# Side work placed anew in a two-layer attention kernel: table portions, block ends, norm steps and an iteration's scaling

## The chip, the core and the metric

The kernel runs on one core of a Trainium2 chip. The metric is device microseconds of one execution. The core has engines that each work through their own list of instructions in order: TensorE (PE in the profile, with PEld for its weight loads), VectorE (DVE), ScalarE (ACT), GpSimd (POOL), and SyncE (SP), which here only issues DMAs. An instruction whose operands are not ready holds up everything behind it on its engine. So the place of an instruction in its engine's list matters as much as its length.

## What is computed

Two layers over x of shape (2, 512, 64, 32), that is 2 batches of 2048 tokens with 512 channels, 8 heads of 64, all in float32:

```python
# layer 0: full attention, q and k with 64 more channels of frequency and time embeddings
q, k = [x, emb] @ Wq, [x, emb] @ Wk;  v = x @ Wv
o = softmax(q k^T / 8) v
x1 = x + o @ Wout + bout
# layer 1: normalization, Nystrom attention (256 landmarks), quantized feed-forward
n = layernorm(x1);  q, k, v = n @ Wqkv
qL, kL = means of 8 tokens each
A = softmax(qL kL^T);  z = 6 steps of an iterative pseudo-inverse of A
o = softmax(q kL^T) (z (softmax(qL k^T) v)) + conv(v)
x2 = x1 + o @ Wout1 + bout1
out = x2 + layernorm(x2) @ (dequantized table @ W)
```

The feed-forward weight is a 512 x 512 array of 4-bit indices into a table of 16 levels, with a scale for 64 elements each. One step of the pseudo-inverse is z <- z (13 - xz (15 - xz (7 - xz))) / 4.

## The kernel before

The tokens of a batch are cut into four blocks of 512, the channels into four chunks of 128 partitions, and the heads are worked in pairs (two heads of 64 fill 128 partitions). There are 8 pairs: two batches of four. The order of the work is written by hand: Python generators yield after each unit of work, and loops advance them at set places. TensorE's list is therefore what the source says, step by step, and so are those of VectorE, ScalarE and GpSimd. The order of SyncE's DMAs is set by a planner.

**First layer.** `attention0` walks the 64 steps of a pair (four blocks of queries times 16 chunks of keys) in groups of two. A group does the scores (L1258), their exponentials on ScalarE (L1266), VectorE's additions for the row sums (L1276), and the values matmuls (L1288) of the group before. Every eight groups a block ends: an addition into q_f (L1295), the row sums on TensorE (L788), a reciprocal (L1303), a DMA that spreads it, and GpSimd's multiplication (L1306).

The next pair's work stands between these groups. At the groups named in `BURSTS[n]` a filler is advanced up to its next REST: projections of q and k (with their combined weights, L989 to L992, and evictions L1018 and L1023), value projections (L1126), and at the end two reductions of |q| and |k| with a bound (L1114, L1116). In any other group one entry of the list `soon` is run (a token sum L900, a finish step), or else one portion of `feed_forward_map`, which makes the feed-forward weight from the table: for each of four chunks a conversion of the indices (L1342 to L1347), 14 levels (a comparison L1352 and an addition L1353), a scaling (L1357); at the end the products mp (L1364) and the store of the result. One portion stood in each such group whose number is not a multiple of 8, and one beside each value projection but those of pair 0.

For n = 4, the first pair of batch 1, the finish of batch 0's first layer is the filler too: out units (matmuls yp_f, eviction into xr_f L1148) and the norm's steps. Those are: sums L1159/L1160, mean L1163, subtraction L1164, squares L1167/L1170 on ScalarE, additions L1175/L1176, variance L1179, square root L1181, reciprocal L1198, and two multiplications, GpSimd's L1201 and VectorE's L1202.

**Between the layers** the string `ORDER` sets the turns: m is one product of the second layer's projections (L2072, eviction L2082), n a norm step, o an out unit.

**Second layer.** The loop `for n, pair in enumerate(todo)` (L2402) runs the pseudo-inverse of one pair. `iteration_start` scales A into M (L1766 to L1774). Each step of `pinv` (L1800) squares M, then R: a flip by TensorE (L1796) that ScalarE copies back (L1797), the products (L1806), and subtractions by VectorE (L1819). Between the steps `chunk(c)` places the next pair's scores and values (attn3, L1635) and the previous pair's last attention (attn1: scores L1863, exponentials L1868, sums L1872, values L1879, row sums L788, reciprocal L1892, L1899, L1900). Between the three last products (wp L1781, tp L1790) `last(i)` places more. In both, `advance(finish)` places single steps of batch 0's or 1's finish: out units yp_g, norm steps as above (reciprocal L1928), and units of the feed-forward fp_g (L1962, with L1951 and L1952). A last string (L2546) sets the turns of the end.

TensorE's results lie in PSUM banks: four in turn for most work (`bank`) and two for the products of the iteration (`product_bank`).

Of the kernel before, what the change touches and what calls it, by code (L numbers as in the profile page):

```python
# [13 lines left out]
ALU = mybir.AluOpType  # L14
# [23 lines left out]
def general_path(  # L38
# [618 lines left out]

BAND = P + 2 * HALO

ORDER = "1mononmmnomomnnm2mnoonmnmnmoonmn3mmnoonmnmmnoommnnmnmmnmmnmmnmmmmnmmmmmn"  # L660

GAP = object()
REST = object()

FEW = (2, 1), (1, 2), (1, 1), (2, 2)
BURSTS = (
    *[(1, 6, 14, 23)] * 3, (4, 10, 17, 25), (1, 3, 6, 10, 12, 15, 18, 20, 23, 26, 28, 31),
    (4, 12, 21), (4, 12, 21), (12, 22),
)

# [2 lines left out]
def fast_path(  # L673
# [241 lines left out]
    class Heads0:  # L915
# [139 lines left out]
        def units(self, xbs, parts, after=None, ready=None):  # L1055

            self.xbs = xbs
            self.begin()
            values = self.values()
            if self.b == 0:  # L1060
                for kind in "q" if self.plain else "qk":
                    self.few(kind)
                self.embed(4)
                yield
                yield REST
            if self.plain:
                for i, (kind, t) in enumerate(self.uses):
                    if i == 2 and self.b == 0:
                        self.few("k")
                        self.embed(2)  # L1070
                    if kind == "q" and self.b:
                        if t == 0:
                            yield from values
                            while not ready():
                                yield GAP
                    if kind == "q" and t == 0:
                        self.queries()
                    self.project(kind, t)
                    yield
                if after:  # L1080
                    after.begin()
            else:
                self.queries()
                if self.b and self.hp == 0:
                    for m in range(2):
                        next(values)
                        yield
                    parts[0].begin()
                    yield REST
                if not self.ws:  # L1090
                    self.combine_w()
                    for _ in range(2):
                        next(values)
                        yield
                while ready and not ready():
                    yield GAP
                for tp in range(2):
                    yield from self.products(tp, parts[tp], parts[1] if tp == 0 else after)
            if self.next:
                self.next.load()  # L1100
                if self.next.b:
                    self.next.embed(4)
            for _ in values:
                if self.hp or self.b:
                    advance(ffn_map)
                yield
                if self.next and not self.next.plain and not self.next.ws:
                    self.next.combine_w()
            if self.next:
                self.next.load("v")  # L1110

            big = small.tile([P, 2], F32, tag="big0", name=f"big_{self.name}")
            for i, m in enumerate((self.q, self.k)):
                nc.vector.tensor_reduce(big[:, i : i + 1], m, AX.X, ALU.max, apply_absolute_value=True)  # L1114
            i = self.b * NPAIR + self.hp
            nc.vector.scalar_tensor_tensor(  # L1116
                bound[:, i : i + 1], big[:, :1], D**-0.5, big[:, 1:], ALU.mult, ALU.mult
            )
            yield

    def values_of_tokens(v, t, xb, w_of, name):

# [123 lines left out]
    def attention0(hd, filler, needed, bursts, beside=None):  # L1246
# [62 lines left out]
        for i in range(0, len(steps) + 1, GROUP):  # L1309
            group = [(step, scores(*step)) for step in steps[i : i + GROUP]]  # L1310
            for step, p in group:
                add(step, p)
            for step, p, its_acc in pending:
                values(step, p, its_acc)
            pending = [(step, p, acc) for step, p in group]
            burst = i // GROUP in bursts
            if burst:
                advance(filler, len(steps), True)
            if not group:
                while needed in filler:  # L1320
                    advance(filler)
            if late:
                sums(*late)
                late = None
            if soon and not burst:
                soon.pop(0)()
            elif beside and not burst and i // GROUP % 8:
                advance(beside)

    def feed_forward_map():  # L1330
# [8 lines left out]
        for k in range(KC):  # L1339
            nc.sync.dma_start(qi, qidx[k * P : (k + 1) * P, :])  # L1340
            yield
            nc.vector.tensor_copy(qf, qi)  # L1342

            nc.vector.tensor_scalar(hits[:, 0, :], qf, 0.0, float(len(NF4)), ALU.is_lt, ALU.mult)
            nc.vector.tensor_tensor(qf, qf, hits[:, 0, :], ALU.add)
            nc.vector.tensor_scalar(qf, qf, 0.0, float(len(NF4) - 1), ALU.max, ALU.min)
            nc.vector.tensor_scalar(wl[:, k, :], qf, 0.0, NF4[0], ALU.is_equal, ALU.mult)  # L1347
            yield
            for i, level in enumerate(NF4):
                if i and level:  # L1350
                    hit = hits[:, i % 4, :]
                    nc.vector.tensor_scalar(hit, qf, float(i), level, ALU.is_equal, ALU.mult)  # L1352
                    nc.vector.tensor_tensor(wl[:, k, :], wl[:, k, :], hit, ALU.add)  # L1353
                yield
            for j in range(C // 64):
                blk = wl[:, k, j * 64 : (j + 1) * 64]
                nc.vector.tensor_scalar(blk, blk, sc_sb[:, k, j : j + 1], None, ALU.mult)  # L1357
        wff_sb = block_of(lpool, "wo", "wff_f")
        nc.sync.dma_start(wff_sb, chunked(wffT))
        yield  # L1360
        for m in range(KC):
            mp = bank(f"mp1_{m}")
            for k in range(KC):
                nc.tensor.matmul(  # L1364
                    mp, lhsT=wl[:, k, m * P : (m + 1) * P], rhs=wff_sb[:, k, :], start=k == 0, stop=k == KC - 1
                )
            nc.scalar.copy(tmp[:, m, :], mp)
            yield
        nc.sync.dma_start(mT_d, tmp)
        yield  # L1370

    def load_wo(w, name):
# [599 lines left out]
    def finish1_units(b, os, early):  # L1972
        for t in range(NTB):
            if t == NTB - 1 and early:
                f = early.pop()
                yield from f.out_units()
                yield from f.norm_units()
                yield from f.map_units(lambda m, name: bank(name))
                return
# [22 lines left out]
        after = parts_for(others[0])[0] if others and not (n and plain(n)) else None  # L2002
        return heads[n].units(xbs, None if plain(n) else parts_for(n), after, ready)

    ffn_map = [feed_forward_map()]
    cur = heads[0]
    cur.w = w0_first
    drain(units_of(0))
# [1 line left out]
    for n, (b, hp) in enumerate(todo[:-1]):  # L2010
# [12 lines left out]
        if n == 3:  # L2023
            while ffn_map:
                advance(ffn_map)
            wo_sb = load_wo(wo0, "wo_f0")
            write_bands()
        if hp == NPAIR - 1:
            last_oTs, oTs = oTs, []
# [368 lines left out]

    finish, early = [], []
    for n, pair in enumerate(todo):  # L2402
        before = todo[n - 1] if n else None
        after = todo[n + 1] if n + 1 < len(todo) else None
# [4 lines left out]
        if n == NPAIR + 3:  # L2409

            xb = as_block(kvpool.tile([P, NST, P], F32, tag="v", name="xb_g_early"))
            xn = lambda: block_of(lpool, "xn", "xn_g_early")
            early.append(Finish1(1, NTB - 1, [p.o for p in todo[:NPAIR]], xb, xn, True))
            before.load_o(late_buffer(f"o2_{n - 1}"))
        pair.iteration_start()
        while vals:
            advance(vals)
        if after:
# [4 lines left out]
        if n:  # L2423
            q = late_buffer if n > NPAIR + 1 else lambda name: kvpool.tile([P, S], F32, tag="k", name=name)
            pair.prefetch1(q(f"q2_{pair.name}"))

        def chunk(c):
            nonlocal landmarks
            if before and 0 < c <= n_ones:
                before.attn1_end(c - 1)  # L2430
            if n == NPAIR and c == 1:

                finish.append(finish1_units(1, [p.o for p in todo[:NPAIR]], early))
            advance(finish)
            if c == NTB:
                if after:
                    landmarks = after.landmarks_values()
                    next(landmarks)
                    drain(convolution(n + 1))
                else:  # L2440
                    advance(finish, 2)
                return
            ones_before = before if c < n_ones else None
            if ones_before:
# [2 lines left out]
                    before.attn1_scores(c, 1)  # L2447
                before.attn1_add(c)
            if after:
                for s, bank_of in ((2 * c, product_bank), (2 * c + 1, bank)):  # L2450
                    after.attn3_scores(s, bank_of)
                    after.attn3_add(s)
            else:
                advance(finish)
            if ones_before:
                before.attn1_values(c)
            if after:
                after.attn3_values(2 * c)
            else:
                advance(finish)  # L2460
            if after:
                after.attn3_values(2 * c + 1)
            if ones_before:
                before.attn1_sums(c)
                before.attn1_inverse(c)
            if n == NPAIR + 2 and c % 2:
                advance(finish)

        def last(i):
            nonlocal start  # L2470
# [24 lines left out]
            if i == 5:  # L2495
                pair.attn1_scores(0, 0)
                pair.attn1_scores(0, 1)
            advance(finish)

        landmarks = start = None  # L2500
        n_ones = NTB if n + 2 < len(todo) else NTB - 1
# [41 lines left out]


    ones_last = last_attn1()
    for c in "1f1ffnf11f1ff1afafff1f1f1f1faas11bs1bs1bbt":  # L2546
        if c == "f":
            advance(finish)
        elif c == "n":
# [111 lines left out]
```

## Time and profile before

| | us |
|---|---|
| median of 3 runs | 2706.99 |
| lowest, highest run | 2700.99, 2707.6 |
| the profiled execution's own time | 2700.81 |
| its span in the profile | 2699.0 |

The mean granted TensorE clock of the profiled execution is 0.997. The stages, with busy times in us (times from the span's start):

| stage | start to end | PE | DVE | ACT | POOL |
|---|---|---|---|---|---|
| first projections | 0 to 56 | 52.2 | 17.4 | 5.6 | 0.2 |
| attention of pair 0 | 56 to 182 | 123.6 | 106.0 | 50.1 | 15.4 |
| pair 1 | 182 to 341 | 153.6 | 137.0 | 66.8 | 17.2 |
| pair 2 | 341 to 500 | 153.7 | 136.2 | 66.6 | 17.7 |
| pair 3 | 500 to 660 | 159.6 | 132.2 | 69.5 | 7.4 |
| pairs 4 to 7 | 660 to 1390 | 723.6 | 497.1 | 304.5 | 45.8 |
| between the layers | 1390 to 1710 | 309.7 | 224.0 | 86.1 | 20.0 |
| iterations of pairs 0 to 5 | 1710 to 2310 | 595.6 | 297.6 | 177.9 | 28.8 |
| pair 6 | 2310 to 2440 | 125.3 | 78.8 | 35.6 | 7.4 |
| pair 7 | 2440 to 2530 | 85.3 | 47.7 | 19.6 | 6.1 |
| the end | 2530 to 2699 | 158.1 | 100.7 | 25.4 | 6.8 |

The profile's rows name a source line, an engine, an operation, and its output and inputs. Row numbers such as L1806 are lines of the kernel before. A bracket at a row's end gives the idle time of that engine just before it and what ended it. Idle time of an engine that isn't the bottleneck costs nothing by itself.

### The profile page before, as it was taken

Reading aid. Unit: us, or ns where it says so; the run is one execution under the profiler, and the core shown is the slowest. Engines: PE = TensorE matmul, PEld = TensorE weight load, DVE = VectorE, ACT = ScalarE, POOL = GpSimd, SP = SyncE. Lnnn points to the kernel's source line nnn. Section 1 sums busy time; section 2 is a strip of 40 time slices with the busy share of each in tenths; the row PEclk is TensorE's granted clock in tenths of the full one; section 3 lists DMA queues with packets and bytes.
Section 4 is the critical chain, followed back from the end, with each engine's and each line's share of the span. In section 5 each row is a group of like instructions: output and inputs, shape, how many; then the busy total and the mean of one; then the engine's idle time right before and its main releaser. Section 6 shows DMA issues by size and latency. Waiting matters only on the chain.

```text
span 2699.0 us, 41317 instructions
## 1 busy us (share of the span) xinstructions
PE 2640.4 (98%) x16898; PEld 1346.8 (50%) x16898; DVE 1774.5 (66%) x2253; ACT 907.5 (34%) x1356; POOL 172.8 (6%) x127
## 2 busy tenths in 40 slices
PE   9999999999999999999999999999999999999998
PEld 5343433444344434343344455777677666655344
DVE  4898888976557677767668856544644645465565
ACT  1344344443343335345422223223333222231210
POOL 0101010000001100000002000000000000000000
PEclk9999999999999999999999999999999999999999
DMA  4101011201221210020114633213111113021211
GB/s 134 38 13 45 13 36 44 75 21 52 86 79 59 78 52 13 24 85 29 45 61 170 229 109 114 90 33 125 49 37 60 61 42 105 28 79 36 90 39 48
DMA packets 124759, 177.16 MB, mean 66 GB/s; under 512 B 16912, under 2 KB 78096, under 8 KB 122000
## 3 DMA queue, kind: packets, MB, share of 16 engines
q1 hardware_dynamic: 118416, 153.15, 18.0%
q0 software_dynamic: 5440, 20.97, 2.1%
q8 instruction: 134, 2.20, 0.3%
q14 instruction: 65, 0.53, 0.1%
q10 hardware_dynamic: 704, 0.31, 0.0%
HBM read 94.02 MB, written 63.57 MB: 58 GB/s over the span
## 4 chain that ended last, share of the span: by engine, by line
PE 85%; DVE 10%; issue 2%; ACT 1%; DMA 1%; SPq 0%; POOL 0%; DVEq 0%; ACTq 0%; POOLq 0%
PE sc_f L1258 13%; PE av_f L1288 13%; PE pa L1806 5%; PE pb L1806 5%; DVE acc_f L1276 5%; PE vp L1126 4%; PE vp_f L1126 4%; PE fp_g L1962 4%; PE yp_g L1141 4%; PE yp_f L1141 3%; PE pc_f L1003 3%; PE pu L2072 3%; PE sc L1863 2%; PE sc L1635 2%; PE av L1656 2%; PE av L1879 2%
## 5 line engine op out<-in xcount | busy, mean ns | idle before, releaser
L1266 ACT ACTIVATE p_f<-sc_f 128x1024 f32<-128x1024 f32 x512 | 496.5, 1021 | 583.2 <-PE sc_f L1258 581.6
L1276 DVE TENSOR_TENSOR acc_f<-acc_f,p_f 128x1024 f32<-128x1024 f32 x448 | 577.0, 1288 | 133.8 <-ACT p_f L1266 106.4
L1258 PE MATMUL sc_f<-q_f,k_f 64*64 64x512 f32 x4096 | 490.4, 593 | 2.6 <-ACT p_f L1266 2.6
L1288 PE MATMUL av_f<-p_f,v_f 64*64 64x512 f32 x4096 | 485.2, 589 | 0.0
L1288 PEld LDWEIGHTS av_f<-p_f,v_f 64*64 64x64 f32 x4096 | 157.0, 133 | 283.1 <-issue 282.4
L1258 PEld LDWEIGHTS sc_f<-q_f,k_f 64*64 64x64 f32 x4096 | 148.5, 133 | 284.3 <-issue 262.6
L1806 PE MATMUL pa<-M 128*128 128x192 f32 (+1 forms) x640 | 153.4, 385 | 5.6 <-ACT M L1797 5.6
L1806 PE MATMUL pb<-R 128*128 128x192 f32 (+1 forms) x640 | 149.3, 380 | 0.0
L1306 POOL TENSOR_TENSOR q_f<-q_f,rinv_f 128x512 f32<-128x512 f32 x32 | 51.2, 1600 | 1123.2 <-DMA rinv_f<-acc_f 880.1
L1806 PEld LDWEIGHTS pa<-M 128*128 128x128 f32 x640 | 109.3, 195 | 27.2 <-ACT M L1797 8.7
L1126 PEld LDWEIGHTS vp_f<-wv_f,x 128*128 128x128 f32 x1024 | 115.7, 192 | 8.9 <-issue 8.9
L1806 PEld LDWEIGHTS pb<-R 128*128 128x128 f32 x640 | 106.6, 190 | 23.3 <-DVE M L1819 0.3
L1141 PE MATMUL yp_f<-q_f,wo_f 128*128 128x512 f32 x256 | 113.2, 596 | 4.2 <-DVE xr_f L1148 4.2
L1126 PE MATMUL vp_f<-wv_f,x 128*128 128x128 f32 x1024 | 117.3, 276 | 0.0
L1141 PE MATMUL yp_g<-o,wo_f 128*128 128x512 f32 x256 | 114.8, 598 | 0.0
L1126 PE MATMUL vp<-w,xh 128*128 128x128 f32 x896 | 105.9, 277 | 0.0
L1126 PEld LDWEIGHTS vp<-w,xh 128*128 128x128 f32 x896 | 102.1, 192 | 4.9 <-issue 3.0
L1819 DVE SCALAR_TENSOR_TENSOR M<-M,pb 128x320 f32<-128x320 f32 (+1 forms) x160 | 60.1, 417 | 60.7 <-PE pb L1806 60.7
L1962 PE MATMUL fp_g<-xn_g,mT 128*128 128x512 f32 (+1 forms) x232 | 99.8, 580 | 0.0
L1900 POOL TENSOR_TENSOR o<-o,rinv 128x512 f32<-128x512 f32 x32 | 46.0, 1436 | 815.8 <-DVE rinv L1899 673.2
L1868 ACT ACTIVATE p<-sc 128x512 f32<-128x512 f32 x128 | 66.6, 602 | 93.4 <-PE sc L1863 93.2
L1819 DVE SCALAR_TENSOR_TENSOR R<-M,pa 128x320 f32<-128x320 f32 (+1 forms) x160 | 58.5, 407 | 49.5 <-PE pa L1806 49.4
(278 smaller groups left out, 3204.4 us busy)
## 6 DMA issues: line engine op xcount, KB each, us to landing
xh<-xh_fd SPq DMA_DIRECT2D x12, 1024.0 KB, 5.9
rinv_f<-acc_f SPq DMA_DIRECT2D x256, 32.0 KB, 1.9
xr_f<-in_x_dram SPq DMA_DIRECT2D x8, 1024.0 KB, 5.1
x_fd<-xr_f POOLq DMA_DIRECT2D x8, 1024.0 KB, 4.9
xh_fd<-xn_f POOLq DMA_DIRECT2D x8, 1024.0 KB, 4.6
k<-k_fd SPq DMA_DIRECT2D x8, 1024.0 KB, 6.1
rinv<-acc SPq DMA_DIRECT2D x256, 32.0 KB, 1.8
x<-in_x_dram SPq DMA_DIRECT2D x7, 1024.0 KB, 6.0
```

The costliest lines, as they stand in the source:

```text
L1003: nc.tensor.matmul(to, lhsT=w[:, k, :], rhs=x[:, k, :], start=start and k == 0, stop=k == 1, skip_group_check=True,)
L1126: nc.tensor.matmul(vp[:, j * P : (j + 1) * P], lhsT=xb[:, k, j * P : (j + 1) * P], rhs=w_of(k), start=k == 0, stop=k == KC - 1,)
L1141: nc.tensor.matmul(yp, lhsT=wo_sb[:, k, m * P : (m + 1) * P], rhs=oTs[k][:, toks], start=k == 0, stop=k == NPAIR - 1,)
L1258: nc.tensor.matmul(sc[r * D : (r + 1) * D, h, :], lhsT=hd.k[rows, lo : lo + D], rhs=hd.q[rows, t * TB : (t + 1) * TB], start=True, stop=True,)
L1266: nc.scalar.activation(p, sc, AF.Exp, scale=D**-0.5)
L1276: nc.vector.tensor_tensor(acc, first if c == 1 else acc, p, ALU.add)
L1288: nc.tensor.matmul(av[r][half, :], lhsT=hd.v[keys, c, half], rhs=pp[keys, h, :], start=c == 0, stop=c == NST - 1,)
L1806: nc.tensor.matmul(dst, lhsT=lhsT[:, k, t * P : (t + 1) * P], rhs=rhs[:, k, :], start=k == 0, stop=k == 1)
L1819: nc.vector.scalar_tensor_tensor(out, m, scale, pr, ALU.mult, ALU.subtract)
L1868: nc.scalar.activation(p[:, h, :], sc, AF.Exp, scale=D**-0.5)
L1962: nc.tensor.matmul(fp[:, cols], lhsT=mT[:, k, m * P : (m + 1) * P], rhs=self.xn[:, k, cols], start=k == 0, stop=k == KC - 1,)
L2072: nc.tensor.matmul(to, lhsT=w[:, k, :], rhs=x[:, k, :], start=start and k == 0, stop=k == 1, skip_group_check=True)
```

## The change

No instruction of arithmetic is added or taken away; the change moves work on the engines' lists, and one choice of banks.

- **Table portions.** A portion stands in the groups of `TABLE` alone, and `NVS` = 3, 3, 3, 1 portions stand beside a pair's four value projections (and three beside each of pair 4's first two). A conversion is two portions. The load of the out weight `wo_f0` stands right behind the store of the finished map.
- **The bound's reductions.** That of |q| stays; that of |k| and the bound go to `soon`.
- **BURSTS[4].** From the fourth burst on, most are one group earlier, so that an out unit stands right behind a block's row sums (groups 9, 17, 25).
- **ORDER.** The same steps in other turns; the last norm's reciprocal and multiplications ahead of two small sums and a weight's combination.
- **TURNS.** Where pairs 4 to 7 of the second layer had a finish step at fixed places, a table says how many (f), and where the out units of the last block (o) stand. The squares no longer stand ahead of a flip's copy.
- **`iteration_start`** of the next pair at the end of the present one, ahead of that turn's finish step.
- **Banks of attn3's scores.** The plain bank first and the product bank second, where it was the other way, if c is 0 or no pair is before.
- **TAIL.** Two letters of the last string move by a few places.

```diff
-ORDER = "1mononmmnomomnnm2mnoonmnmnmoonmn3mmnoonmnmmnoommnnmnmmnmmnmmnmmmmnmmmmmn"
+ORDER = "1omnonmmnomomnnm2mnoonmnmnmoomnnm3mnoonmnmmnoomnnmnmmmnmnmmmnmmmmnmnmmmm"
+TURNS = (
+    (",,,", "f,,,", "f,,,", "f,,,", "f,", "f,f,f,f,f,"),
+    ("f,,,", "ff,,,", "f,,,", "f,,,", "f,", "f,f,f,f,f,f"),
+    ("fff,,,", "ff,,,", "f,,,", "f,,,", "ff,", ",f,f,f,f,"),
+    ("fffoo,,,", "f,f,f,", "f,f,f,", "ff,,oo,", "f,", ",f,,f,f,ff"),
+)
+TAIL = "11fffnf11f1ff1afafff1f1f1f1faas11bsbs11bbt"
+TABLE = 9, 10, 11, 12, 16, 17, 18, 19, 20, 21, 22, 25, 27
+NVS = 3, 3, 3, 1
...
-    *[(1, 6, 14, 23)] * 3, (4, 10, 17, 25), (1, 3, 6, 10, 12, 15, 18, 20, 23, 26, 28, 31),
+    *[(1, 6, 14, 23)] * 3, (4, 10, 17, 25), (1, 3, 6, 9, 11, 14, 17, 19, 22, 25, 27, 30),
...
                     for m in range(2):
                         next(values)
+                        advance(ffn_map, 3)
                         yield
...
-            for _ in values:
-                if self.hp or self.b:
-                    advance(ffn_map)
+            for i, _ in enumerate(values):
+                advance(ffn_map, NVS[i])
                 yield
...
+            def most(i, m):
                 nc.vector.tensor_reduce(big[:, i : i + 1], m, AX.X, ALU.max, apply_absolute_value=True)
+            def both_of_them():
+                most(1, self.k)
...
+            most(0, self.q)
+            soon.append(both_of_them)
...
-            elif beside and not burst and i // GROUP % 8:
+            elif beside and not burst and i // GROUP in TABLE:
                 advance(beside)
...
             nc.vector.tensor_tensor(qf, qf, hits[:, 0, :], ALU.add)
+            yield
...
         nc.sync.dma_start(mT_d, tmp)
+        loaded.append(load_wo(wo0, "wo_f0"))
...
-        pair.iteration_start()
+        if not n:
+            pair.iteration_start()
...
+        def turn(c, i):
+            for turn in TURNS[n - NPAIR][c].split(",")[i] if n >= NPAIR else "":
+                if turn == "f":
+                    advance(finish)
+                else:
+                    next(outs_early[0])
...
-            advance(finish)
+            turn(c, 0)
...
-                for s, bank_of in ((2 * c, product_bank), (2 * c + 1, bank)):
+                kinds = (product_bank, bank) if c and before else (bank, product_bank)
+                for s, bank_of in zip((2 * c, 2 * c + 1), kinds):
...
                 pair.attn1_scores(0, 1)
-            advance(finish)
+                if after:
+                    after.iteration_start()
+            turn(NTB + 1, i)
...
-    for c in "1f1ffnf11f1ff1afafff1f1f1f1faas11bs1bs1bbt":
+    for c in TAIL:
```

More of the change, by code (lines that the diff above doesn't have):

```diff
@@ L1112, in units @@
             big = small.tile([P, 2], F32, tag="big0", name=f"big_{self.name}")
-            for i, m in enumerate((self.q, self.k)):
+            def most(i, m):
                 nc.vector.tensor_reduce(big[:, i : i + 1], m, AX.X, ALU.max, apply_absolute_value=True)
[L1115 to L1119, printed above, removed]
+            def both_of_them():
+                most(1, self.k)
+                i = self.b * NPAIR + self.hp
+                nc.vector.scalar_tensor_tensor(
+                    bound[:, i : i + 1], big[:, :1], D**-0.5, big[:, 1:], ALU.mult, ALU.mult
+                )
+            most(0, self.q)
+            soon.append(both_of_them)
     def values_of_tokens(v, t, xb, w_of, name):
@@ L1360, in feed_forward_map @@
         yield
+        yield
+        yield
         for m in range(KC):
@@ L1975, in finish1_units @@
                 f = early.pop()
-                yield from f.out_units()
+                yield from outs_early[0]
                 yield from f.norm_units()
@@ L2003, in units_of @@
         return heads[n].units(xbs, None if plain(n) else parts_for(n), after, ready)
-    ffn_map = [feed_forward_map()]
+    loaded, ffn_map = [], [feed_forward_map()]
     cur = heads[0]
@@ L2025, in fast_path @@
                 advance(ffn_map)
-            wo_sb = load_wo(wo0, "wo_f0")
+            wo_sb = loaded.pop()
             write_bands()
@@ L2397, in fast_path @@
     todo[0].prefetch1(kvpool.tile([P, S], F32, tag="k", name="q2_first"))
-    finish, early = [], []
+    finish, early, outs_early = [], [], []
     for n, pair in enumerate(todo):
@@ L2413, in fast_path @@
             early.append(Finish1(1, NTB - 1, [p.o for p in todo[:NPAIR]], xb, xn, True))
+            outs_early.append(early[0].out_units())
             before.load_o(late_buffer(f"o2_{n - 1}"))
-        pair.iteration_start()
+        if not n:
+            pair.iteration_start()
         while vals:
@@ L2439, in chunk @@
                     drain(convolution(n + 1))
-                else:
-                    advance(finish, 2)
+                turn(c, 1)
                 return
@@ L2449, in chunk @@
             if after:
-                for s, bank_of in ((2 * c, product_bank), (2 * c + 1, bank)):
+                kinds = (product_bank, bank) if c and before else (bank, product_bank)
+                for s, bank_of in zip((2 * c, 2 * c + 1), kinds):
                     after.attn3_scores(s, bank_of)
                     after.attn3_add(s)
-            else:
-                advance(finish)
+            turn(c, 1)
             if ones_before:
@@ L2458, in chunk @@
                 after.attn3_values(2 * c)
-            else:
-                advance(finish)
+            turn(c, 2)
             if after:
@@ L2465, in chunk @@
                 before.attn1_inverse(c)
-            if n == NPAIR + 2 and c % 2:
-                advance(finish)
+            turn(c, 3)
         def last(i):
@@ L2497, in last @@
                 pair.attn1_scores(0, 1)
-            advance(finish)
+                if after:
+                    after.iteration_start()
+            turn(NTB + 1, i)
         landmarks = start = None
```

## The prediction

> **What bounds the kernel now.** First the page's busy times, then TensorE's waits by releaser, then the timeline at each wait.
>
> ```profile
> PE 2640.4 (98%) x16898; PEld 1346.8 (50%) x16898; DVE 1774.5 (66%) x2253; ACT 907.5 (34%) x1356; POOL 172.8 (6%) x127
> ```
>
> TensorE (PE) is busy for 2640.4 of 2699.0 us at a mean granted clock of 0.997. The change adds and removes no arithmetic, so it can only win from TensorE's idle time, 50.9 us between matmuls and 7.8 us behind the last, and from matmuls that ran at a low clock. The rest of this text is about whom TensorE waits for (total us, times, longest):
>
> ```profile
> PE pc_f L1003 <- DVE k_f L1018: 9.7, 7, 2.9
> PE pa L1806 <- ACT M L1797: 5.6, 2, 4.2
> PE yp_f L1141 <- DVE xr_f L1148: 4.2, 2, 2.1
> PE rs_f L788 <- DVE acc_f L1276: 3.5, 3, 2.1
> PE wp L1781 <- DVE R L1819: 3.2, 2, 2.1
> ...
> PE sc L1550 <- DVE L L1518: 2.5, 1, 2.5
> PE sc L1635 <- DVE M L1819: 2.2, 10, 0.2
> ```
>
> Nearly all are waits for VectorE (DVE) which has work in front of what TensorE needs, though it is busy for only 66% of the span: an order too late, not an engine too small. Below, "->" is from a wait before to my wait after, in us.
>
> **Table portions, reduces, bursts (first layer).** A steady group of two steps costs TensorE 3.43 us (four batches near 1.7) and VectorE two adds, 2 x 1.29 less overlap = 2.48, so a group has 0.95 free. A level (L1352 + L1353) costs 1.07 from start to start, more than the 0.95: portions in consecutive groups make a backlog, and the next burst of projections waits for its k_f eviction. Value projections (14.6 us of TensorE each head) leave VectorE idle:
>
> ```profile
> 168.37 0.42 DVE L1352 TENSOR_SCALAR hits_f<-tmp_f 128x512 f32<-128x512 f32 x1
> 168.82 0.69 DVE L1353 TENSOR_TENSOR wl_f<-wl_f,hits_f 128x512 f32<-128x512 f32 x1
> ...
> 173.02 2.28 DVE L1114 TENSOR_REDUCE big_f<-q_f 128x1 f32<-128x2048 f32 x1
> ...
> 181.83 1.23 DVE L1276 TENSOR_TENSOR acc_f<-p_f,p_f 128x1024 f32<-128x1024 f32 x1 [4.14 <-ACT p_f L1266]
> ```
>
> The 4.14 at the end is VectorE idle before the first add. The change puts ten portions here: for head 0's end 6 levels (6.42), the weight combination (1.47), a scaling (1.30), a conversion (2.45) and one reduce (2.20) make 13.84, ending at 182.2 against 181.83: 0.4 late. The k reduce with its bound (2.44) follows in the next free group, against four levels fewer later (4.28).
> - Heads 0 to 2, bursts at group 6 in heads 1 and 2: 2.93 and 2.67 -> 0, since no portion is left in groups 1 to 8 (before: one in each free group). Bursts at 14: 1.61, 0.90, 0.22 -> 0: one portion less (1.07) and its free 0.95 make 2.0 us.
> - Head 0, group 6: the k reduce now stands in group 5 behind the token sums: 0.78 -> 3.2. A loss.
> - Row sums at the ends: 1.24 -> 0.5, 2.15 -> 0.15, 0.16 -> 0.
> - Together 12.66 -> 3.85: **8.8 us**. The table's beginning beside head 0's own values costs nothing: VectorE was idle there for 8.73 us before the first add at 56.0.
> - Head 4: the out projections wait (2.13, 2.10) for xr_f evictions behind the reciprocal L1198 (3.33). One group earlier, L1198 falls in the idle time before the row sums, and the out unit has some 1.2 us to spare: -> 0. Of 0.56, 0.11 and 0.62 there remains 0.28. **5.2 us**. SP's wo_f load moves ahead of the loop's end, right behind the table's store; in that queue row-sum spreads stand behind it, but its buffer's last readers (the mp matmuls) are done before the store, so it holds nobody.
>
> **ORDER between the layers.** Moving one pu or eviction ahead empties 1.60 and 0.14; mean and part come 1.1 us sooner for the sc wait (2.53 -> 1.4), and 2.24 -> 1.75. 1.26, 0.86, 0.56 and 0.99 keep their releasers. [...]
>
> ```profile
> 1473.19 3.38 POOL L1201 TENSOR_TENSOR xn_f<-xn_f,rstd_n 128x1024 f32<-128x1024 f32 x1 [12.62 <-DVE rstd_n L1198]
> 1474.28 2.44 DVE L1518 TENSOR_SCALAR L<-L 128x256 f32<-128x256 f32 x1
> ```
>
> L1518 alone takes 0.29 (at 1478.48); beside GpSimd's multiply it ends only when that does. [...] then bringing L1198 and L1202 forward brings the block (2.15) with them, whatever stands behind it pays, and 2.24 stays 2.24 (part: 2.8 us). By the row of a conversion beside GpSimd in head 1 (four instructions 0.7 to 0.85 late each, no full block) half would go, 1.1 (part: 3.9). I take 0.5: **3.3 us**, ends 1 and 5.
>
> **Score banks and scaling.** Ten waits of 0.22 (sc L1635) are for the bank that the last product still holds; the first score then takes a fresh one: **2.2 us**, ends 0 and 2.2. The next iteration's scaling (L1770 to L1774, 1.6 us of VectorE) stands ahead of the finish step L1148, which waited for its projection: 1.20 -> 0, **1.2 us**. Behind it nothing is late: that turn ends with matmuls of 3.7 us.
>
> **Finish steps by table.** The largest single wait:
>
> ```profile
> 2482.74 2.28 DVE L1164 TENSOR_TENSOR xn_g<-xb_g,mean_g 128x2048 f32<-128x2048 f32 x1
> 2485.05 1.06 ACT L1167 ACTIVATE sq_g<-xn_g 128x1024 f32<-128x1024 f32 x1 [5.45 <-DVE xn_g L1164]
> 2486.01 1.13 ACT L1170 ACTIVATE sq_g<-xn_g 128x512 f32<-128x512 f32 x2
> 2487.05 0.24 ACT L1797 COPY M<-p_pa 128x128 f32<-128x128 f32 x1
> 2487.35 1.44 PE L1806 MATMUL pa<-M 128*128 128x320 f32 x2 [4.22 <-ACT M L1797]
> ...
> 2488.79 3.62 PE L1806 MATMUL pa<-M 128*128 128x192 f32 x8
> ```
>
> ScalarE (ACT) serves in order: the squares wait for L1164, and the 0.24 us flip copy that the iteration needs stands behind them. In the changed program squares come one chunk later, behind a flip copy, and two out units of the last block (7.4 us of matmuls) cover L1164: 4.22 -> 0. The matmuls behind took 3.62 where they take 1.89 elsewhere; with the next ones 2.6 us are lost to the clock. The windows show it:
>
> ```profile
> 240.00:246.00 6.00, 4.89 (x12) 2.17 (x13) 3.73 (x6) 0.00 (x0) 3.07 (x3) 1.00 0.14 51
> 2488.00:2493.00 5.00, 5.00 (x16) 3.76 (x15) 1.96 (x6) 0.53 (x2) 0.00 (x0) 0.56 0.00 0
> ```
>
> (start:end, length, busy times, then granted clock, DMA share, GB/s). A wait of 2.93 left the clock at 1.00, 4.22 brought 0.56. [...] But behind the 2.53 wait at 1478.83 the clock was 0.60, and about 1.5 us went. [...]
> - Pair 4 to 5: squares off the flip, 1.43 -> 0.
> - Pair 6: the squares' adds (1.28 + 0.69) leave the place before R, and L1928 (3.35) no longer stands before R's subtraction: 2.06 + 1.19 -> 0, less 0.5 for a chunk in which VectorE has 8.4 us of work against 8.7.
> - Pair 7, gains: 4.22 + 2.6. New waits: its fp units no longer stand between wp and tp, so the two later wp each wait for the add or the subtraction, 0.75 + 0.75. The variance now stands just ahead of the last block's scores: sqrt (0.69) with a table load (1.28) before and after it keeps ScalarE from the exponentials, and the fourth score needs the bank that the first one frees: 1.25. Net 4.05.
> - Together 1.4 + 2.75 + 4.05 = **8.2 us**, ends 3 and 10.
>
> **Tail string.** Two waits, 1.56 (rinv behind L1159/L1160) and 1.51 (var_g), -> one of 1.45: the mean's matmul, now right behind the scores, waits for the last fp unit's two additions and L1159/L1160: **1.6 us**. From 2600 on nothing moves, and the 7.8 us end stays.
>
> **Sum.** 8.8 + 5.2 + 3.3 + 2.2 + 1.2 + 8.2 + 1.6 = 30.5 us. The profiled execution took 2700.81 us (span 2699.0 and 1.8 around it): 2670.3. The runs shown lie at 2700.99, 2706.99 and 2707.6, so the profiled one is like the lowest; I put the forecast 3 us above the sum, half way to the median's 6: **2673 us**, 1.2% less.
>
> **Rivals.**
> - *The cover doesn't hold in the iterations* (pairs 5 to 7): the new waits of pair 7 and pair 6 eat all 8.2, with the scaling's 1.2, and bursts of heads 0 to 2 keep half (4.4): 30.5 - 13.8 = 17 us, 2684 to 2690. For it: in pair 7 three waits are added by hand count. Against: the larger waits go for a reason seen in the trace.
> - *The waits only move*: behind each wait removed the next releaser is as late. Less than 8 us, 2693 to 2707. For it: VectorE is 88 to 98% busy in the second to fourth slices of the page. Against: in the value projections it idles for 4 us.
> - *Slower: a VectorE backlog at the twelve bursts and row sums of heads 0 to 2.* Portions now stand at groups 16 to 22 in a row and at 25 and 27; with the k reduce put into a free group, a backlog of one level and one reduce (1.07 + 2.44 = 3.5) may reach TensorE each time. It decides from about 3.6 us each: 12 x 3.6 = 43 against 12.66 before eats the 21.7 of the other parts and 9 more. Beyond 4.2 each would add 2.6 of clock, 12 x 6.8 = 82: 2748. Against: groups 5 to 8 and 13 to 15 are free to recover 0.95 each.
> - *It does not do what it says*: the instruction order of the two programs excludes this; every move above stands in it.
>
> **Chances.** Forecast 0.66 (2662 to 2682); iteration cover fails 0.18; waits move 0.10; slower 0.05; larger gain than all ends 0.01. A measurement of this kernel tells some 0.3%, 8 us, from no change. Faster 0.85, same 0.10, slower 0.05. The low end is the sum of the upper ends (30.5 + 1.5 + 1.7 + 1.8 + some of the 3.85 left = 38) from the lowest run of 2701, some 2662, and 1 below it; the upper end takes in the first rival: 2692.
>
> **What will show it.** No wait of pc_f for k_f over 1 us after 200 us; pc_f at about 80 us near 3; no pa wait for ACT M; sc L1635 gone from the list; clock 1.00 around 2460; waits of wp for R near 0.75 twice and one of sc for the exponentials near 1.25 in pair 7. A TensorE idle sum over 40 us would make me wrong, or one at the low clock.

## The result

| | before, us | changed, us |
|---|---|---|
| median of 5 runs each (before: the 3 shown ahead and 2 more) | 2704.54 (2700.99 to 2707.6) | 2663.84 (2662.55 to 2665.19) |
| profiled execution, its span | 2700.81, 2699.0 | 2662.55, 2660.7 |
| TensorE idle up to its last matmul, summed over the trace | 50.9 | 20.5 |
| TensorE busy | 2640.4 | 2632.5 |

The ratio is 0.9849 (95% interval 0.9835 to 0.9864). The forecast was 2673 us in a range of 2661 to 2692, so it was right in its sign and its range, and 9 us short. The page's busy times after, and TensorE's waits by releaser (us in total, times, longest):

```profile
PE 2632.5 (99%) x16898; PEld 1345.3 (51%) x16898; DVE 1770.9 (67%) x2253; ACT 907.7 (34%) x1356; POOL 171.7 (6%) x127
```

```profile
PE pc_f L1014 <- DVE k_f L1029: 3.2, 2, 3.0
PE pu L2093 <- DVE s L1499: 2.3, 3, 1.1
...
PE mean_g L1180 <- DVE xn_g_early L1177: 1.5, 1, 1.5
PE sc L1884 <- ACT p L1889: 1.5, 2, 0.8
...
PE wp L1802 <- DVE R L1840: 0.8, 2, 0.4
```

Line numbers of the changed kernel are 11 to 21 higher: pc_f L1014 was L1003. Seven waits of pc_f became two, one of them the 3.0 of head 0, where 3.2 was forecast; the wait of pa for ScalarE's flip copy is gone, and so are yp_f's and the long ones of wp. Of the ten waits of sc L1635 nine are gone; the tenth (now L1656, 0.22 at 2348) stands in a last chunk, where the banks were not swapped. The instructions that count as busy are the same in number on each engine, so the 38.3 us come from two sources: 30.4 of idle time and 7.9 of busy time. The second is where the forecast was short.

To see where the time went, TensorE's two lists were laid side by side, and the clock time of the same count of matmuls was compared. The difference is the second column; the third is from the experiments, each of which takes the part back, compared with the changed kernel in the same way, with the start of the span left out.

| part | forecast | traces, before to after | part taken back |
|---|---|---|---|
| first layer: portions, reduces, bursts | 14.0 | 12.6 | 15.7 |
| ORDER | 3.3 | 5.5 | 7.3 |
| score banks | 2.2 | 6.3 | 6.3 |
| scaling, finish steps, last string | 11.0 | 12.7 | 14.4 |
| start (x arriving) | 0 | 1.1 | |
| sum | 30.5 | 38.2 | |

The start is no doing of the change: the first waits for the time embedding and for x are 0.67 and 1.42 before, 0.36 and 0.35 after, and one and the same program below started once with none and once with 1.44. The third column adds up to more than the second because three of the four kernels met low clocks that the kernel before had not met at those places, some 1.6 us each; the section on the clock shows such falls.

### The profile page after: what moved, and what is told of

It reads as the page before. It is cut to its first block, busy times and chain, and to the rows that moved or that the text cites. A ratio compares the mean times of both kernels' runs of the same rounds, so it can differ in the third digit from the quotient of the medians.

```text
span 2660.7 us, 41330 instructions
## 1 busy us (share of the span) xinstructions
PE 2632.5 (99%) x16898; PEld 1345.3 (51%) x16898; DVE 1770.9 (67%) x2253; ACT 907.7 (34%) x1356; POOL 171.7 (6%) x127
## 4 chain that ended last, share of the span: by engine, by line
PE 93%; DVE 4%; ACT 1%; issue 1%; DMA 1%; SPq 0%; DVEq 0%; ACTq 0%
PE sc_f L1275 16%; PE av_f L1305 15%; PE pb L1827 5%; PE pa L1827 5%; PE vp_f L1143 4%; PE yp_g L1158 4%; PE fp_g L1983 4%; PE yp_f L1158 4%; PE vp L1143 4%; PE pc_f L1014 3%; PE pu L2093 3%; PE sc L1656 2%; PE pu_f L1014 2%; PE sc L1884 2%; PE av L1677 2%; PE pp L1478 2%
## 5 line engine op out<-in xcount | busy, mean ns | idle before, releaser
L1921 POOL TENSOR_TENSOR o<-o,rinv 128x512 f32<-128x512 f32 x32 | 45.3, 1416 | 797.6 <-DVE rinv L1920 652.6
```

## The experiments

**Each part taken back.** Four kernels, each the changed kernel with one part as it was before. All four together give the kernel before, instruction by instruction.

```diff
# banks_back
-                kinds = (product_bank, bank) if c and before else (bank, product_bank)
+                kinds = product_bank, bank
# heads_back
-    *[(1, 6, 14, 23)] * 3, (4, 10, 17, 25), (1, 3, 6, 9, 11, 14, 17, 19, 22, 25, 27, 30),
+    *[(1, 6, 14, 23)] * 3, (4, 10, 17, 25), (1, 3, 6, 10, 12, 15, 18, 20, 23, 26, 28, 31),
...
-                advance(ffn_map, NVS[i])
+                if self.hp or self.b:
+                    advance(ffn_map)
...
-            soon.append(both_of_them)
+            both_of_them()
...
-            elif beside and not burst and i // GROUP in TABLE:
+            elif beside and not burst and i // GROUP % 8:
...
# order_back
-ORDER = "1omnonmmnomomnnm2mnoonmnmnmoomnnm3mnoonmnmmnoomnnmnmmmnmnmmmnmmmmnmnmmmm"
+ORDER = "1mononmmnomomnnm2mnoonmnmnmoonmn3mmnoonmnmmnoommnnmnmmnmmnmmnmmmmnmmmmmn"
# turns_back
...
-            turn(c, 0)
+            advance(finish)
...
-                if after:
-                    after.iteration_start()
-            turn(NTB + 1, i)
+            advance(finish)
...
```

> The changed kernel with the banks of attn3's scores as before. Gap theory (the prediction's): only the ten waits of 0.22 us return, the span is 2.2 us longer than the changed kernel's 2660.7. Run-out theory: each wait also makes the two matmuls ahead of it run out (0.70 us for a pair before, where the whole group of 16 now takes 2.04 against 2.91 with the wait), so each costs 0.87, and the span is 5 to 8 us longer.

Median 2669.92 us, ratio to the kernel before 0.9870 (0.9851 to 0.9889), span 2670.0. Of the 9.3 us more of span, 2.2 lie at the start and in head 0's slow matmuls, and 6.3 at the nine waits that are back: four of 0.50 in the first pair and five of 0.86. The rest is spread in steps of 0.4 and less. The timeline of TensorE in this kernel at one such place, and of the changed kernel at the same place:

```profile
1877.94 0.70 PE L1656 MATMUL sc<-L,k 64*128 64x256 f32 x2
1878.85 1.99 PE L1656 MATMUL sc<-L,k 64*128 64x256 f32 x14 [0.22 <-DVE M L1840]
```

```profile
1872.75 2.04 PE L1656 MATMUL sc<-L,k 64*128 64x256 f32 x16
```

The wait's own row says 0.22. But the sixteen matmuls take 0.70 + 0.22 + 1.99 = 2.91 us with the wait and 2.04 without it: 0.87. In the row of sixteen, with no idle time in it, two matmuls take about 0.26 (2.04 / 8); ahead of the wait the two are shown with 0.70. So 0.44 of the price stands in the busy time ahead of the wait, and 0.2 in that behind it (14 matmuls in 1.99, where 14/16 of 2.04 is 1.79). The run-out theory holds here, and the gap theory falls.

> The changed kernel with the first layer's parts as before (portions, k reduce, bursts, load of the out weight). Gap theory: the 12.66 and 5.5 us of waits return for those left, span 14.0 us longer. Run-out theory: the same gaps, 0.27 more at each pc wait and the 1.7 us of slow matmuls behind the new wait of 2.98 gone: 12 to 13 us longer.

Median 2679.73 us, 0.9910 (0.9890 to 0.9929), span 2676.6. The waits of before are back one by one (1.61, 1.23, 2.93, 1.09, 2.14, 2.69, 2.12, 2.10, 0.62), and the one at 82 us is 0.77 again. The sum is 15.7 us and thus above both theories; 3.4 of it are slow matmuls behind the two waits of 2.1, which before had not been slow.

> The changed kernel with the string between the layers as before. Gap theory: 3.3 us longer. Clock theory: besides the gaps (4.1 in the traces) the matmuls behind the wait for L are slow again, 1.4 more: 5 to 6 us longer, and a granted clock of about 0.6 for the 3 us behind that wait. If the clock there stays at 1.00 with the wait back, the clock was chance.

Median 2670.18 us, 0.9869 (0.9850 to 0.9889), span 2669.3. The string costs 7.3 us, more than both: waits of 1.61, 2.53 and 2.24 are back, the clock falls to 0.60 behind the second and, as it had not before, to 0.62 behind the third (means over windows of 3.4 us, as are the clocks given for single places below).

> The changed kernel with the iteration's finish steps, the next iteration's scaling and the last string as before. Gap theory with the clock of the 4.22 wait: 8.2 + 1.2 + 1.6 = 11.0 us longer. Run-out theory: the traces' sum over these stages, 12.5 to 13.5 us longer, with 0.3 to 0.5 hidden in the matmuls ahead of each of the eight waits.

Median 2675.58 us, 0.9892 (0.9873 to 0.9911), span 2675.8. 14.4 us: above the gap theory's 11.0, and 1 over the run-out theory's. The 4.2 wait and its low clock are back, and so is the 2.06 of wp, here with a clock of 0.56 that it had not brought before.

**The k reduce.** Pair 0 alone, and then every pair, with the k reduce and the bound at once instead of in a free group:

```diff
# pair0_k_at_once
-            soon.append(both_of_them)
+            if self.b or self.hp:
+                soon.append(both_of_them)
+            else:
+                both_of_them()
# k_at_once
-            soon.append(both_of_them)
+            both_of_them()
```

> The changed kernel, with the k reduce and the bound of pair 0 alone made at once, beside its own value projections, where VectorE waits 4.13 us for the first exponentials. If the reduce in group 5 is the cause of the 2.98 wait at 82 us, that wait falls to 0.8 as before, and the clock behind it (0.72 to 0.78, some 1.7 us) comes back: 3 to 4 us off the span. If the token sums are the cause, the wait stays near 3.

Median 2661.87 us, 0.9837 (0.9821 to 0.9854), span 2657.7: 3.0 us less than the changed kernel's (by the medians 2.0; in head 0 the traces differ by 3.9, and the start and later waits take 0.8 back). The timelines of the changed kernel, then of this one, ahead of the burst at group 6:

```profile
76.65 2.28 DVE L1126 TENSOR_REDUCE big_f<-k_f 128x1 f32<-128x2048 f32 x1
...
78.97 0.16 DVE L1131 SCALAR_TENSOR_TENSOR bound<-big_f 128x1 f32<-128x1 f32 x1
79.04 2.55 DVE L1293 TENSOR_TENSOR acc_f<-acc_f,p_f 128x1024 f32<-128x1024 f32 x2
...
81.51 0.69 DVE L1029 TENSOR_TENSOR k_f<-pc_f,e_k_f 128x512 f32<-128x512 f32 x1
82.25 2.99 PE L1014 MATMUL pc_f<-t,s_f 128*128 128x512 f32 x4 [2.98 <-DVE k_f L1029]
```

```profile
79.12 0.68 DVE L1029 TENSOR_TENSOR k_f<-pc_f,e_k_f 128x512 f32<-128x512 f32 x1
79.86 1.98 PE L1014 MATMUL pc_f<-t,s_f 128*128 128x512 f32 x4 [0.77 <-DVE k_f L1029]
```

The reduce with the bound, 2.44 us, stands ahead of the last additions and of the k_f eviction; without it the wait falls from 2.98 to 0.77 and the matmuls behind from 2.99 to 1.98. The rest of the 3.9 are the matmuls that follow at a low clock in the changed kernel (0.66 from 82 to 87) and not here. The reduce was the cause, the token sums were not.

> The changed kernel, with the k reduce and the bound of every pair made at once. By the prediction's count (13.84 us of VectorE work ending 0.4 late, and 2.44 more with this) the row sums and first additions at the ends of heads 0 and 1 come 2 us later than in the changed kernel: rs waits of 1.2 to 2.5 where it has 0.23 and 0.35; head 0's wait is 0.8 as in the run for pair 0 alone. If VectorE's idle time there is larger than counted, the rs waits stay under 0.5 and the deferral was worth nothing.

One run, 2664.59 us, span 2662.7. Head 0's wait is 0.78, but at the ends of heads 0 and 1 there are new ones of 1.46 and 1.21, of the values matmul for VectorE's L1312 and not of the row sums. From 180 to 530 us this kernel loses 5.2 us to the changed one, where the run for pair 0 alone loses 0.6. So putting the reduce off was worth some 4.6 us at the ends of the heads, and cost 3.9 in pair 0, whose own values have no next head behind them.

**Pair 7 and the tail.**

```diff
# var_behind_scores: TURNS, pair 7, last row
-",f,,f,f,ff"
+",f,,f,,fff"
# tail_out_first
-TAIL = "11fffnf11f1ff1afafff1f1f1f1faas11bsbs11bbt"
+TAIL = "11fffnf11af1ff1fafff1f1f1f1faas11bsbs11bbt"
```

> The changed kernel, with pair 7's variance step behind the last block's scores and not ahead of them. If the sqrt and its table loads are the cause of the two waits of 0.46 and 0.79 in those scores, both go and the span is 1.3 to 2 us shorter; if the wait is for a bank that another reader holds, about 1 us stays.

One run, 2662.31 us, span 2660.4. In that stage it wins 1.1 us, and the start takes 0.7 back. Both waits in the scores are gone, so the variance's place ahead of the scores, with its sqrt between two table loads, was their cause. In the changed kernel's timeline (ScalarE and the scores' matmuls):

```profile
2482.91 1.28 ACT L1198 ACT_TABLE_LOAD   x1
...
2484.20 0.69 ACT L1198 ACTIVATE rstd_g<-var_g,eps 128x512 f32<-128x512 f32 x1
2484.91 1.28 ACT L1889 ACT_TABLE_LOAD   x1
...
2484.94 1.12 PE L1884 MATMUL sc<-q,L 64*128 64x512 f32 x2 [0.46 <-ACT rstd_g L1198]
2486.20 1.57 ACT L1889 ACTIVATE p<-sc 128x512 f32<-128x512 f32 x3
2486.85 1.12 PE L1884 MATMUL sc<-q,L 64*128 64x512 f32 x2 [0.79 <-ACT p L1889]
```

The third score waits for the variance's bank until the sqrt has read it, the fourth for the bank that the first exponential frees. But waits of 0.80 (tp for ScalarE's copy of R) and 0.63 (row sums) have come in their place: the variance's matmuls had covered the first of them.

> The changed kernel, with the first out unit of the last string moved ahead of the mean. Its 3.6 us of matmuls cover the 1.54 us that the mean's matmul waits for L1177; the variance behind has 3.6 us less cover and waits some 0.5. About 1 us shorter; if the variance then waits 1.5 or more, nothing is won.

One run, 2665.56 us, span 2663.8, which is 3.1 us longer: a miss. The wait for L1177 is gone, and the out unit in front of it waits 1.53 us for GpSimd's o (L1921) instead. In this run the clock was also at 0.52 from 2489 on, behind waits of under 0.8 alone, which cost 1.7. The moved unit alone costs some 0.5; the rest of the 3.1 lies mostly at the start.

**The clock, and all together.**

> The kernel before once more, for a second look at the clock. If the clock falls by a fixed length of the wait, the same places as in the first look fall again and no others: behind the waits of 2.53 (1479) and 4.22 (2487), with 1.00 behind 2.93, 2.67 and 2.13. [...]

> The kernel with the first layer's parts as before, once more. Fixed length: clock 0.6 behind the two waits of 2.1 at 824 and 880 as in its first look, 1.00 behind 2.93 at 240 and 2.69 at 400. [...]

2704.27 us with a span of 2702.5, and 2678.06 with 2676.2. The windows of the kernel before, in its first and its second execution (start:end, length, busy times of PE, PEld, DVE, ACT, POOL, granted clock, DMA share, GB/s), at the waits of 2.93, 2.1, 2.1 and 2.53:

```profile
240.00:246.00 6.00, 4.89 (x12) 2.17 (x13) 3.73 (x6) 0.00 (x0) 3.07 (x3) 1.00 0.14 51
824.00:830.00 6.00, 5.11 (x12) 2.39 (x13) 2.24 (x4) 0.00 (x0) 0.18 (x1) 1.00 0.46 175
880.00:886.00 6.00, 6.00 (x15) 2.47 (x13) 0.75 (x1) 0.00 (x0) 0.00 (x0) 1.00 0.29 109
1478.00:1484.00 6.00, 5.17 (x14) 2.75 (x15) 5.58 (x7) 2.48 (x4) 0.00 (x0) 0.72 0.86 282
```

```profile
240.00:246.00 6.00, 5.53 (x10) 2.46 (x11) 2.71 (x5) 0.00 (x0) 2.23 (x3) 0.72 0.12 44
825.00:831.00 6.00, 5.08 (x8) 2.20 (x9) 1.52 (x3) 0.00 (x0) 0.21 (x1) 0.72 0.46 175
881.00:887.00 6.00, 5.16 (x8) 2.26 (x9) 1.44 (x3) 0.00 (x0) 0.13 (x1) 0.72 0.46 175
1482.00:1488.00 6.00, 4.50 (x16) 2.06 (x16) 5.96 (x7) 2.09 (x3) 0.05 (x1) 1.00 0.90 295
```

The same waits in the same program, and all four have changed sides (1.00 against 0.72). In the two executions of heads_back three of four have (0.72 against 1.00 again): slow at 824 and 880 and not at 240, then slow at 240 and not at 826 and 880. So a fixed length of the wait did not decide. What a fall costs was nearly the same each time: 1.5 to 1.7 us of longer matmuls in the stage concerned (in heads_back the row of yp_f at 824 takes 8.83 where it takes 7.13 before). At 1479 of the kernel before it cost nothing on balance: without it, in the second execution, the matmuls were 1.5 shorter and the next waits longer by as much (for kq 2.25 where 1.26 was, and 0.27 more), and the two were level again. The 4.2 wait was followed by a low clock in each of the three executions that have it (0.50 from 2485.56 to 2492.39 in the first of the kernel before), and the 2.98 of head 0 in each of the six that have it (means of 0.50 to 0.85 from 85.0 to 88.4).

The traces' clock records give the length of a fall. In the first execution of the kernel before the clock is 0.50 for 3.41 us from 1478.63 and for 6.83 us from 2485.56, in the changed kernel for 3.41 us from 83.08. Windows of 3.41 us, in the first execution at 240 and at 1479 (both pairs counted in such steps from the fall at 1478.63), and in the second at 240, ahead of the fall and on it:

```profile
236.18:239.59 3.41, 2.00 (x5) 0.57 (x3) 3.27 (x5) 0.00 (x0) 0.00 (x0) 1.00 0.00 0
239.59:243.01 3.42, 1.90 (x5) 0.94 (x6) 2.16 (x3) 0.00 (x0) 1.05 (x1) 1.00 0.00 0
1475.22:1478.63 3.41, 1.08 (x3) 0.19 (x1) 3.38 (x4) 0.00 (x0) 2.14 (x2) 1.00 0.24 87
1478.63:1482.04 3.41, 3.21 (x10) 1.88 (x11) 3.41 (x5) 0.52 (x2) 0.00 (x0) 0.50 0.97 325
```

```profile
236.66:240.07 3.41, 0.88 (x3) 0.05 (x1) 3.31 (x4) 0.00 (x0) 0.00 (x0) 1.00 0.00 0
240.07:243.49 3.42, 3.02 (x4) 1.47 (x5) 1.04 (x2) 0.00 (x0) 1.05 (x1) 0.50 0.20 77
```

The length less the first busy time is TensorE's idle time in the window. It is 2.33 us ahead of the fall at 1478.63 and 2.53 ahead of the one at 240.07; ahead of the fall at 2485.56 it is 2.43 (2482.15 to 2485.56, busy for 0.98), and ahead of the changed kernel's at 83.08 it is 2.58 (79.67 to 83.08, busy for 0.83). Of the 2.93 at 240 in the first execution, 1.41 and 1.52 stand in the two windows shown, and the clock was 1.00 in both. Against these stands the fall from 2489 on in tail_out_first, behind waits of under 0.8 alone. What decides between a fall and none was not shown. By an estimate from the records, a fall of 3.41 us at 0.50 costs at most half of that, 1.7 us.

> The changed kernel with three edits: pair 0's k reduce at once, pair 7's variance behind the scores, and the small sums csum copied by ScalarE instead of VectorE. The first two took 3.0 and about 1 us in their own runs: span near 2656.5. On the third: [...] with the copies gone the next reduce runs beside GpSimd and the wait of 0.60 for s at 1484 us falls to 0. If the reduce is blocked as well, the 0.60 stays.

The edit that is new here:

```diff
-            nc.vector.tensor_copy(csum[:, i, 2 * h : 2 * h + 2], a[:, :, LM])
+            nc.scalar.copy(csum[:, i, 2 * h : 2 * h + 2], a[:, :, LM])
```

Median 2658.48 us (2657.73 to 2659.11), ratio to the kernel before 0.9832 (0.9819 to 0.9846), span 2656.7. It is the fastest of all, 5.4 us below the changed kernel's median; the two were not timed side by side, and the intervals of their ratios overlap, though their runs do not. The wait for s is gone. VectorE beside GpSimd's multiply of 3.3 us, first in the kernel before (where the addition for s stands behind the multiply), then in the changed kernel, then here:

```profile
1499.44 3.30 POOL L1201 TENSOR_TENSOR xn_f<-xn_f,rstd_n 128x1024 f32<-128x1024 f32 x1 [21.78 <-DVE rstd_n L1198]
1500.46 2.56 DVE L1478 TENSOR_TENSOR s<-s,w 128x256 f32<-128x256 f32 x1
```

```profile
1478.42 3.31 POOL L1218 TENSOR_TENSOR xn_f<-xn_f,rstd_n 128x1024 f32<-128x1024 f32 x1 [17.41 <-DVE rstd_n L1215]
1479.44 1.27 DVE L1595 TENSOR_REDUCE rsum<-X 128x2 f32<-128x512 f32 x2
...
1480.63 1.20 DVE L1620 COPY csum<-A 128x2 f32<-128x2 f32 x2
1481.75 1.21 DVE L1528 TENSOR_REDUCE L<-kq 128x128 f32<-128x1024 f32 x1
```

```profile
1475.50 3.32 POOL L1221 TENSOR_TENSOR xn_f<-xn_f,rstd_n 128x1024 f32<-128x1024 f32 x1 [17.42 <-DVE rstd_n L1218]
1476.52 1.27 DVE L1598 TENSOR_REDUCE rsum<-X 128x2 f32<-128x512 f32 x2
1477.71 1.21 DVE L1531 TENSOR_REDUCE L<-kq 128x128 f32<-128x1024 f32 x1
```

The reduces took the same while GpSimd worked (1.27 for the two of rsum and 1.21 here) as where it is idle (1.27 at 1492.56 and 1.21 at 1494.47 before). The two copies of two columns, 0.16 and 0.17 where GpSimd is idle (at 1493.75 and 1494.40 before), took 1.20, until 1481.83, and GpSimd's multiply ended at 1481.73. In the kernel before it was the addition for s itself that lasted so long: 2.56, until 1503.02 where the multiply ended at 1502.74, and 0.42 where GpSimd is idle (at 1483.32 in the changed kernel).

## Why the forecast was right, and where it was short

- **The likeliest case came.** The time went where the forecast had it: TensorE's idle time fell by 30.4 us, and the forecast's sum of waits, without the 2.6 us of clock, is 27.9.
- **First layer, 14.0: came at 12.6.** The waits left in heads 0 to 2 were put at 3.85 and are 2.98 + 0.23 + 0.35 + 0.24 = 3.80; head 4 keeps 0.70 where 0.28 was said. The term came out lower for a reason that the forecast had left to its range, at 2.6 us: behind the 2.98 the clock fell (to 0.50 from 83.08 to 86.50), at 1.7 us.
- **ORDER, 3.3: mis-sized, 5.5.** The wait for L was put at 1.4 and is 0.37, that for s at 1.75 and is 0.60; against it a wait of 1.15 has come that I had not seen, of a pu whose s now stands behind the subtraction L1181 (2.29). "Whatever stands behind it pays" was too blunt: beside GpSimd's multiply the addition for s (2.56 against 0.42), the two copies of csum (1.20 against 0.16 and 0.17) and L1539 (2.45 against 0.29, as before) lasted until about its end, the reduces (1.27 and 1.21) took the same as without it, and at the second multiply the reduces now stand where the addition for s stood. The row of head 1 that the forecast took for "no full block" does not speak against this: GpSimd's additions there take 1.04 each alone, so 0.7 to 0.85 late is less than one of them. The idle time makes 4.1 of the 5.5; the other 1.4 stand as slow matmuls behind the 2.53, which I had counted at nothing since the wait of 2.93 had cost none, with 1.5 left to the range. The second execution of the kernel before shows that they are no price of their own: with the clock at 1.00 there, the next waits took their place.
- **Score banks, 2.2: mis-sized, 6.3.** The mechanism is right and the price is 0.50 (four times, in the first pair) to 0.86 (five) for a wait shown as 0.22; the tenth wait stayed. This is the largest miss: the forecast took the idle column for the whole price of a wait.
- **Scaling, finish steps and string, 11.0: 12.7.** The pa wait of 4.22 and its slow matmuls are gone as said. Of pair 7's new waits, the scores' 1.25 is 0.46 + 0.79 = 1.25 and the two of wp are 0.39 and 0.38, half of the 0.75 each. The tail's remaining wait was put at 1.45 and is 1.54. The 0.5 that pair 6 was to pay did not come. These make 1.1 of the 1.7; that the rest is run-out ahead of the waits removed is likely and not shown.
- **The median.** I put the forecast 3 us above the sum, since the runs of before lay up to 7 us above the profiled one. That spread belonged to the kernel before: its waits between 2 and 3 us cost clock in one execution and not in the other (at 1479 in the first, at 240, 825 and 881 in the second). Its second execution had a span 3.5 us longer than the first, and its three falls in heads 1 and 4 cost 1.5 to 1.7 each. The mean granted clock of the runs on record goes with it: 0.997 at 2700.72 us, 0.994 at 2709.53. The changed kernel, with one such wait left, spreads by 2.6 us over five runs. Of the 9 us, the parts make 6.6, the start 1.1, and what was put on top for the spread some 1.4.
- **The rivals.** The cover in the iterations holds but for 2.0 us of waits in pair 7. That waits only move is seen in small (1.15 in ORDER; and 0.80 and 0.63, and 1.53 in the two pair 7 and tail experiments), not in the whole. The backlog at twelve places came at one, the one that was counted.

## What to carry to other kernels

A wait on a busy engine can cost more than its idle time, here 0.50 to 0.86 us for one shown as 0.22: add what the last instructions ahead of it take longer, by comparing the same group with and without the wait. Where side work is placed by hand, put it beside long stretches that its engine does not serve, and look at what stands in its queue between the wait's releaser and the work: one reduce of 2.3 us in a group with 0.95 to spare showed up whole at the next burst. Look at the spread too: here waits of 2 to 3 us were followed by a fall of the clock in one execution and not in another, at 1.5 to 1.7 us each, and five runs lay within 6.6 us before and within 2.6 with one such wait left.

## What the runs showed of the hardware

- The granted clock fell to 0.50 for 3.41 us from 1478.63 and for 6.83 us from 2485.56 in the kernel before, and for 3.41 us from 83.08 in the changed kernel. The 3.41 us ahead of these falls held 2.33, 2.43 and 2.58 us of idle time. The waits of 2.93, 2.1, 2.1 and 2.53 were each followed by a fall in one of the two executions of the kernel before and not in the other, the wait of 4.2 in all three executions that have it. A fall cost 1.5 to 1.7 us of longer matmuls, and on balance nothing at 1479. I had counted none behind the waits of 2 to 3 us. What decides, and what set off the fall behind waits of under 0.8 in tail_out_first, was not shown.
- Beside a GpSimd multiply of 3.3 us VectorE's reduces took 1.27 and 1.21, as without it; two copies of two columns took 1.20 against 0.16 and 0.17, an addition of two inputs 2.56 against 0.42 and a tensor_scalar 2.45 against 0.29, each until about the multiply's end.
